# A two-layer graph kernel: projections as three float32r passes instead of seven-product float32 blocks

## The chip, the cores and the metric

The kernel runs on one core of one Trainium2 chip. The metric is the device time of one execution in microseconds (us): the median of three runs before the change is 3069.6 us. A core has five engines that work through queues of their own and wait for each other by semaphores. TensorE (PE in the profile, PEld for its weight loads) multiplies matrices into PSUM. VectorE (DVE), ScalarE (ACT) and GpSimd (POOL) work elementwise. SyncE (SP) issues most of the DMAs.

## The reference, cut to what matters

```python
# x: (64, 256, 512) float32; adj: (256, 256) of 0 and 1
# layer 0: a graph layer
mi = einsum('bkd,od->bko', x, Wi); mj = einsum('bkd,od->bko', x, Wj)
h  = layernorm(x + deg * (mi + b) + einsum('ij,bjo->bio', adj, mj))
# layer 1: attention of 8 heads of 64, masked by adj
q, k, v = h @ Wq.T + bq, h @ Wk.T + bk, h @ Wv.T + bv
attn = softmax(where(adj == 0, -inf, q @ k.T / 8))
out  = layernorm(h + (attn @ v) @ Wo.T + bo)
```

There are 64 elements in the batch. The two 512x512 weights of layer 0 and the four 512x512 projections of layer 1 are most of the arithmetic.

## The kernel before, in words

The kernel takes two elements at a time, so it has 32 groups (`NB` is 2, `NG` is 32), and `for g in range(NG - 1)` runs 31 times. The Python loop is unrolled: one iteration overlaps the attention of group g with layer 0 of group g + 1, and then with the output projection of g and the q, k and v projections of g + 1. Nothing is planned at run time. Matmuls, and whatever is wrapped in `in_order`, stay in the order in which the program emits them. The other instructions are emitted in the same place, and each engine takes its queue from the front.

**Layer 0** (`l0_steps`) makes the products of one element from seven block products (Strassen's scheme, in the form of Winograd). Each product is two float32 matmuls of 128x512. The blocks of x are turned on VectorE by `turn_x`, and their sums come from `sum_x`. The neighbour product (`neighbours`) multiplies the adjacency with `mj`, which was split into two float32r parts, `hi` by ScalarE and `lo` by GpSimd (`split`): eight float32r matmuls of 128x512. The layer norm is `norm_stats` on VectorE, a power on GpSimd (`rstd`) and `norm_apply` on ScalarE. `send_h` writes h to DRAM in columns and reads it back as `hB`, and `turn_h` turns it on VectorE.

**Projections.** `block_product` issues four float32 matmuls of 128x256. `pair_steps` uses it seven times for each of q, k, v and o, so that a projection of two elements takes 28 matmuls. VectorE makes the block sums that these products need (`hS`, `oS`), and it combines the products afterwards. The weight blocks stream in as 256 KB factors: `bring` issues the next one as soon as one has been used.

**Attention** goes over eight head pairs of a group. `scores` makes the scores of one pair: VectorE adds the mask, ScalarE takes exponentials, GpSimd adds the two halves into `pk`. `values` multiplies with v, `divide_two` makes denominators on PE (`den`), reciprocals on VectorE (`rden`), spreads them with eight small DMAs, and `multiply` applies them on GpSimd.

The end of an iteration sets the order of the work around the change:

```python
divide_two(g, w + 1)
run([o[0], neighbours, take1, take0, q[0], give1, send1, o[1], k[0], give0, send0, multiply,
     *left_steps(oS[g], in_order), q[1], k[1]])
run(o[2:6] + work[SLOTS + 2] + [v[0], o[6], v[1]])
```

Here `o[0]` is the first block product of the output projection, which stands ahead of the second element's neighbour product. In the last attention step before it, four layer 0 products of the second element (`q[3:7]`) stand between the scores and the values.

Of the kernel before, what the change touches and what calls it, by code (L numbers as in the profile page):

```python
# [16 lines left out]
P = 128  # L17
# [207 lines left out]
def unshifted_path(ctx, tc, flag, x, adj, wiT, wjT, b0, wqT, bq, wkT, bk, wvT, bv, woT, bo, out):  # L225
# [27 lines left out]
    AHEAD = 8  # L253
# [6 lines left out]
    p4 = ctx.enter_context(tc.tile_pool(name="p4", bufs=4))  # L260
    p6 = ctx.enter_context(tc.tile_pool(name="p6", bufs=6))
    stream = ctx.enter_context(tc.tile_pool(name="stream", bufs=AHEAD + 1))
# [35 lines left out]
    def load_x(b):  # L298
        if b < B:
            xh[b] = p6.tile([P, NT, D], F32, tag="xh", name="xh")  # L300
            nc.sync.dma_start(out=xh[b], in_=x[b].rearrange("(t p) d -> p t d", p=P))

    b_bc = p4.tile([P, D], F32, tag="u", name="b_bc")
# [20 lines left out]
    xT, xS, hT, hS, qT, kT, vv, aoT, oS = ({} for _ in range(9))  # L324


    ident = const.tile([P, P], F32, name="ident")
# [15 lines left out]
    aT = p3.tile([P, NT, N], F32, tag="pk", name="aT")  # L343
    deg = small.tile([P, NT], F32, tag="deg", name="deg")
# [16 lines left out]
    def check_graph():  # L361


        exact = p1.tile([P, NT, N], F32, tag="oS", name="exact")
        in_order(nc.vector.tensor_tensor(exact, aT, graph.bitcast(F32), ALU.not_equal))
        in_order(nc.vector.tensor_reduce(inexact, exact.rearrange("p t n -> p (t n)"), AX.X, ALU.max))
        in_order(nc.vector.tensor_scalar(maskT, aT, 0.0, MASK, ALU.is_equal, ALU.mult))
# [9 lines left out]
    def load_bias(b, name):  # L377
        t = const.tile([P, NC], F32, tag=name, name=name)
        nc.sync.dma_start(out=t, in_=b)
        d = const.tile([P, 2], F32, tag=name + "d", name=name + "d")  # L380
        return t, d

    bq_sb, bqd = load_bias(bq, "bq")
    bk_sb, bkd = load_bias(bk, "bk")

    def bias_steps():
        for t, d in ((bq_sb, bqd), (bk_sb, bkd)):
            in_order(nc.vector.tensor_sub(d, t[:, 2:4], t[:, 0:2]))

    bv_t = small.tile([P, NC], F32, tag="bvt", name="bv_t")  # L390
# [5 lines left out]
    def blocks_of(w):  # L396
        return (w.rearrange("(h c p) (j o) -> p h c j o", h=2, p=P, j=2) if w is woT else
                w.rearrange("(p h c) (j o) -> p h c j o", h=2, p=P, j=2))

    sources = {}  # L400
    for name, w in (("wq", wqT), ("wk", wkT), ("wv", wvT), ("wo", woT)):
        src = blocks_of(w)
        sources[name] = {B11: src[:, 0, :, 0], B21: src[:, 1, :, 0], B22: src[:, 1, :, 1]}


    def load_raw(w, tag):
        raw = p1.tile([P, 2, 2, 2, H], F32, tag=tag, name="raw")
        nc.sync.dma_start(out=raw.rearrange("p h c j o -> p (h c) (j o)"),
                          in_=w.rearrange("(c p) o -> p c o" if w is woT else "(p c) o -> p c o", p=P))
        return raw  # L410

    def make_factors(w, name, raw):
        kept = dram.tile([4, P, 2, H], F32, tag=name, name=name)
        t1, t2, t3, t4 = (p4.tile([P, 2, H], F32, tag="u", name="t") for _ in range(4))
        b11, b12, b21, b22 = (raw[:, h, :, j, :] for h in range(2) for j in range(2))
        for n, (t, p, m) in enumerate(((t1, b12, b11), (t2, b22, t1), (t3, b22, b12), (t4, b21, t2))):
            in_order(nc.vector.tensor_sub(t, p, m))
            nc.sync.dma_start(out=kept[n], in_=t)
        sources[name].update({T1: kept[0], T2: kept[1], T3: kept[2], T4: kept[3]})

    spread = p3.tile([P, NC, P], F32, tag="pk", name="spread")
# [3 lines left out]

    def fold_value_bias(raw):

        pb = score_bank("pb")
        for c in range(NC):
            h, kc = divmod(c, 2)  # L430
            matmul(pb, spread[:, c], raw[:, h, kc].rearrange("p j o -> p (j o)"),
                   start=(c == 0), stop=(c == NC - 1))
        nc.vector.tensor_add(bo_bc, pb, bo_bc)
# [4 lines left out]
    def bring():  # L438
        if queue:
            name, n = queue.pop(0)  # L440
            f = stream.tile([P, 2, H], F32, tag="factor", name="factor")
            nc.sync.dma_start(out=f, in_=sources[name][n])
            coming.append(f)

    def next_factor():
        f = coming.pop(0)
        bring()
        return f


    def norm_stats(t, order=anywhere):
# [3 lines left out]
        nc.vector.bn_aggr(mv, st)  # L455
        ve = small.tile([P, 1], F32, tag="ve", name="ve")
        nc.vector.tensor_scalar(ve, mv[:, 1:2], EPS, None, ALU.add)
# [3 lines left out]
        nc.gpsimd.tensor_tensor(rstd, ve, mhalf, ALU.pow)  # L461
# [40 lines left out]
    def l0_steps(b, late=False):  # L502
# [21 lines left out]
        def split(t):  # L524
            nc.scalar.copy(k["hi"][:, t, :], k["mj"][:, t, :])
            nc.gpsimd.tensor_tensor(k["lo"][:, t, :], k["mj"][:, t, :], k["hi"][:, t, :].bitcast(F32),
                                    ALU.subtract)

        def step1():
            product("x", raw(0, 0), B11, True)  # L530
            nc.scalar.copy(keeper("u1"), banks["x"])

        def step2():
            product("w", raw(1, 1), T4, True)
            add_scaled(1, banks["w"])

        def step3():
            product("x", raw(0, 1), B21, False)
            add_scaled(0, banks["x"])

        def step4():
            product("y", xS[b]["S2"], T2, True)
            nc.vector.tensor_add(keeper("u2"), banks["y"], k["u1"])

        def step5():
            product("z", xS[b]["S1"], T1, True)
            k["mj"] = p1.tile([P, NT, D], F32, tag="mj", name="mj")
            nc.vector.tensor_copy(k["mj"][:, 1, :], banks["z"])

        def step6():  # L550
            product("y", xS[b]["S3"], T3, False)
            nc.vector.tensor_add(keeper("u3"), banks["y"], k["u1"])
            nc.gpsimd.tensor_tensor(k["mj"][:, 1, :], k["mj"][:, 1, :], k["u3"], ALU.add)
# [21 lines left out]
        def take(t):  # L575
            r = xh[b][:, t, :]
            if late and t == 1:
                in_order(add_scaled(1, k["u3"]))
            in_order(nc.vector.tensor_add(r, k["pa"][:, t, :], r))
            stats[t] = norm_stats(r, in_order)  # L580

        def give(t):
            norm_apply(xh[b][:, t, :], *stats[t], in_order)


        return [step1, step2, step3, step4, step5, step6, step7, neighbours, lambda: take(1), lambda: take(0),
                lambda: give(1), lambda: send_h(b, 1), lambda: give(0), lambda: send_h(b, 0)]

    def new_h(g):
        hT[g] = p1.tile([P, NC, NB * N], F32, tag="hT", name="hT")  # L590
        hS[g] = pair_blocks(hT[g], "hS")

    def sum_h(g):
        for step in left_steps(hS[g], in_order):
            step()
# [3 lines left out]
    def send_h(b, t):  # L599
        i = b % NB  # L600
        if t == 1:
            h_cols[b] = dram.tile([D // P, N, P], F32, tag=f"h{i}", name="h_cols")
        nc.sync.dma_start(out=h_cols[b][:, t * P:(t + 1) * P, :].rearrange("q p n -> p q n"),
                          in_=xh[b][:, t, :].rearrange("p (q n) -> p q n", n=P))
        if t == 0:
            hB[b] = p1.tile([P, N // R, P], F32, tag="hB", name="hB")
            nc.sync.dma_start(out=hB[b].rearrange("p a n -> p (a n)"),
                              in_=h_cols[b].rearrange("q (r a) n -> (q r) (a n)", r=R))

    def turn_h(b):  # L610
        g, i = divmod(b, NB)
        if i == 0:
            new_h(g)
        transposed(hT[g][:, :, i * N:(i + 1) * N], hB.pop(b))
        if i == NB - 1:
            sum_h(g)

    def h_transpose(b, t, borrow=False):
# [499 lines left out]
```

## Time and profile before

| what | value |
|---|---|
| median of three runs | 3069.6 us (3069.17 to 3071.52) |
| the profiled execution: own time, span | 3068.79 us, 3066.9 us |
| granted TensorE clock | 0.999 |
| PE, PEld busy | 99%, 69% |
| DVE, ACT, POOL busy | 71%, 32%, 50% |
| DMA share, all 16 engines (queue q1) | 48.8%, 444.5 MB |
| one group, start to start | 94.39 us (1513.37 to 1607.76) |

The span runs from the first to the last instruction, and the execution's own time lies 1.9 us above it. An instruction group of the profile is given as line, engine, operation, output and inputs, count, busy time and mean duration. Ends of matmuls are modelled and overlap, so the time that a matmul really takes is read from the distance of two starts.

### The profile page before, as it was taken

Reading aid. Unit: us, or ns where it says so; the run is one execution under the profiler, and the core shown is the slowest. Engines: PE = TensorE matmul, PEld = TensorE weight load, DVE = VectorE, ACT = ScalarE, POOL = GpSimd, SP = SyncE. Lnnn points to the kernel's source line nnn. Section 1 sums busy time; section 2 is a strip of 40 time slices with the busy share of each in tenths; the row PEclk is TensorE's granted clock in tenths of the full one; section 3 lists DMA queues with packets and bytes.
Section 4 is the critical chain, followed back from the end, with each engine's and each line's share of the span. In section 5 each row is a group of like instructions: output and inputs, shape, how many; then the busy total and the mean of one; then the engine's idle time right before and its main releaser. Section 6 shows DMA issues by size and latency. Waiting matters only on the chain. (4 is left out here: it accounts for less than half of the span.)

```text
span 3066.9 us, 46810 instructions
## 1 busy us (share of the span) xinstructions
PE 3036.6 (99%) x16646; PEld 2124.6 (69%) x16646; DVE 2178.3 (71%) x3298; ACT 974.1 (32%) x1861; POOL 1519.5 (50%) x1255
## 2 busy tenths in 40 slices
PE   7999999999999999999999999999999999999998
PEld 4667766677766777666776667776677766677665
DVE  6776677766777667777677777677766777767775
ACT  2323333323333333332233332333333333323332
POOL 2544545544545445464454554454544546445453
PEclk9999999999999999999999999999999999999999
DMA  7455544455444555345553445544455444555333
GB/s 255 123 151 159 169 121 136 132 161 166 144 125 127 159 170 155 116 133 154 161 168 119 126 145 160 167 134 134 127 158 170 151 121 128 159 161 166 120 111 96
DMA packets 410411, 447.54 MB, mean 146 GB/s; under 512 B 40896, under 2 KB 300224, under 8 KB 409792
## 3 DMA queue, kind: packets, MB, share of 16 engines
q1 hardware_dynamic: 410176, 444.50, 48.8%
q8 instruction: 136, 2.23, 0.3%
q14 instruction: 99, 0.81, 0.1%
HBM read 340.79 MB, written 70.25 MB: 134 GB/s over the span
## 5 line engine op out<-in xcount | busy, mean ns | idle before, releaser
L461 POOL TENSOR_TENSOR rstd<-ve,mhalf 128x1 f32<-128x1 f32 x256 | 140.5, 552 | 707.3 <-DVE below L459 707.3
L816 POOL TENSOR_TENSOR pk<-pe 128x512 f32<-128x512 f32 x256 | 323.1, 1278 | 322.2 <-ACT pe L813 322.2
L290 PE MATMUL po<-w,xS 128*128 128x512 f32 x1024 | 462.2, 599 | 0.7 <-DVE xS L478 0.7
L290 PE MATMUL st<-hS,factor 128*128 128x256 f32 x2048 | 453.2, 379 | 1.5 <-DVE u L689 1.2
L290 PEld LDWEIGHTS st<-hS,factor 128*128 128x128 f32 x2048 | 388.4, 190 | 56.3 <-DVE xh L744 1.7
L813 ACT ACTIVATE pe<-pe 128x1024 f32<-128x1024 f32 x256 | 270.8, 1058 | 364.4 <-DVE pe L809 364.4
L290 PE MATMUL po<-w,xT 128*128 128x512 f32 x768 | 352.1, 601 | 14.8 <-DVE xS L477 9.3
L290 PE MATMUL st<-hT,factor 128*128 128x256 f32 x1536 | 352.5, 379 | 0.7 <-ACT hT L626 0.7
L290 PEld LDWEIGHTS po<-w,xS 128*128 128x128 f32 x1024 | 189.6, 190 | 235.6 <-issue 206.3
L809 DVE TENSOR_TENSOR pe<-ps,maskT 128x1024 f32<-128x1024 f32 x256 | 298.0, 1195 | 35.4 <-PE ps L290 35.4
L290 PEld LDWEIGHTS st<-hT,factor 128*128 128x128 f32 x1536 | 291.9, 190 | 41.8 <-ACT hT L626 0.9
L886 DVE RECIPROCAL rden<-den 128x256 f32<-128x256 f32 x127 | 222.5, 1752 | 76.6 <-PE den L290 73.6
L290 PEld LDWEIGHTS po<-w,xT 128*128 128x128 f32 x768 | 144.2, 191 | 181.9 <-issue 162.8
L887 POOL TENSOR_TENSOR rtot<-rtot,rden 128x256 f32<-128x256 f32 x127 | 106.8, 841 | 320.1 <-DVE rden L886 320.1
L290 PE MATMUL ps<-qT,kT 64*128 64x256 f32 x2048 | 265.0, 393 | 0.0
L290 PE MATMUL pav<-pe,v_sb 128*32 128x256 f32 x4096 | 248.4, 382 | 1.9 <-ACT pe L813 1.9
L290 PEld LDWEIGHTS ps<-qT,kT 64*128 64x128 f32 x2048 | 184.5, 186 | 78.1 <-issue 38.6
L744 DVE TENSOR_TENSOR xh<-st,xh 128x512 f32<-128x512 f32 x186 | 144.5, 777 | 132.2 <-PE st L290 132.2
L290 PE MATMUL st<-factor,hS 128*128 128x256 f32 x1024 | 234.8, 382 | 0.0
L290 PEld LDWEIGHTS pav<-pe,v_sb 128*32 128x32 f32 x4096 | 119.8, 110 | 164.3 <-issue 95.4
L290 PE MATMUL st<-factor,oS 128*128 128x256 f32 x992 | 224.2, 379 | 0.0
L290 PEld LDWEIGHTS st<-factor,hS 128*128 128x128 f32 x1024 | 192.1, 190 | 35.2 <-issue 10.6
(115 smaller groups left out, 4648.2 us busy)
## 6 DMA issues: line engine op xcount, KB each, us to landing
xB<-in_x_dram SPq DMA_DIRECT2D x256, 128.0 KB, 3.9
xh<-in_x_dram SPq DMA_DIRECT2D x64, 512.0 KB, 4.2
factor<-wq SPq DMA_DIRECT2D x128, 256.0 KB, 4.2
factor<-wk SPq DMA_DIRECT2D x128, 256.0 KB, 2.8
factor<-wv SPq DMA_DIRECT2D x128, 256.0 KB, 2.6
spread<-rden SPq DMA_DIRECT2D x1016, 32.0 KB, 1.9
factor<-wo SPq DMA_DIRECT2D x124, 256.0 KB, 3.2
h_cols<-xh SPq DMA_DIRECT2D x124, 256.0 KB, 3.0
```

Of the source, the lines that this page charges most:

```text
L290: in_order(nc.tensor.matmul(*args, **kw))
L461: nc.gpsimd.tensor_tensor(rstd, ve, mhalf, ALU.pow)
L744: nc.vector.tensor_add(dst, src, dst)
L809: nc.vector.tensor_add(pe.rearrange("p j t q -> p j (t q)"), ps.rearrange("p j t q -> p j (t q)"), maskT.rearrange("p t q -> p (t q)").uns ...
L813: in_order(nc.scalar.activation(flat, flat, AF.Exp, scale=QSCALE, accum_out=etot[:, NB * g + i, pr:pr + 1]))
L816: nc.gpsimd.tensor_tensor(pk, pe[:, :, 0, :], pe[:, :, 1, :], ALU.add)
L886: nc.vector.reciprocal(rden, den)
L887: nc.gpsimd.tensor_tensor(rtot, rtot, rden, ALU.add)
```

## The change

The four projections of layer 1 no longer use seven block products. Each operand is split into a head that float32r holds and a small low part. Three float32r matmuls replace one float32 matmul: head by head and low by low into a bank X, and a difference by a difference into a bank Y. The result is X times a constant plus Y. The activations are split on the chip: `split_head` on ScalarE, `split_diff` on VectorE, `split_low` on VectorE or GpSimd. The weights are split once, in `make`, and kept in DRAM. A factor is now 128 x 3 x 512 numbers (768 KB), and six of them are in flight instead of nine of 256 KB. The block sums of h and of the attention output are gone.

Around the products the order changes too. The last attention step keeps two layer 0 products (`q[5:7]`) where four stood. The neighbour product of the second element follows the denominators with nothing between. After it come three layer 0 products of the group two on (`p[0]`, `p[1]`, `p[2]`), and then the output projection, which needs the split attention output.

```diff
-    AHEAD = 8
+    RING = 6
+    UP, DOWN, LIFT = 1 + 2.0 ** -12, 1 - 2.0 ** -13, 2.0 ** 12
...
-            f = stream.tile([P, 2, H], F32, tag="factor", name="factor")
-            nc.sync.dma_start(out=f, in_=sources[name][n])
+            f = stream.tile([P, 3, D], F32R, tag="factor", name="factor")
+            if first:
+                make(f, name, j)
+            else:
+                nc.sync.dma_start(out=f.bitcast(F32), in_=kept[name][j])
...
+            low = nc.vector if late and t == 0 else nc.gpsimd
+            order(low.tensor_tensor(k["lo"][:, t, :], k["mj"][:, t, :], k["hi"][:, t, :].bitcast(F32),
+                                    ALU.subtract))
...
+    def split_head(parts, src):
+        in_order(nc.scalar.activation(parts[0], src, AF.Identity, scale=DOWN))
+
+    def split_diff(parts, src):
+        in_order(nc.vector.scalar_tensor_tensor(parts[2], parts[0].bitcast(F32), UP, src, ALU.mult, ALU.subtract))
+
+    def split_low(parts, src, engine):
+        in_order(engine.tensor_tensor(parts[1], src, parts[0].bitcast(F32), ALU.subtract))
...
+    def rows_of_product(banks, parts, t, f, c):
+        X, Y = banks
+        head, low, diff = (d[:, c, t * P:(t + 1) * P] for d in parts)
+        first, end = c == 0, c == NC - 1
+        matmul(X, head, f[:, 0, :], start=first, stop=False, skip_group_check=True)
+        matmul(Y, diff, f[:, 2, :], start=first, stop=end, skip_group_check=True)
+        matmul(X, low, f[:, 1, :], start=False, stop=end, skip_group_check=True)
...
+            dst = store[g][:, m, :]
+            in_order(nc.scalar.activation(dst, X, AF.Identity, bias=bias[:, m:m + 1], scale=UP))
+            in_order(nc.vector.tensor_add(dst, Y, dst))
...
+            now, later = scores(g, w + 2), scores(g, w + 3)
+            now()
+            if w == NB * NC - 4:
+                head, = three(("qT",))
+                split_head([head[:, :, :N]], aoT[g][:, :, :N])
+            later()
...
+            else:
+                run(q[5:7])
         w = NB * NC - 2
         values(g, w)
         values(g, w + 1)
+        diff, low = three(("kT", "v"))
+        aoP[g] = head, low, diff
+        split_low(*ao_parts(g, 0, every), nc.gpsimd)
         multiply()
...
+        rden = divide_two(g, w + 1)
+        nb2()
+        add2(1)
+        add2(0)
+        split_head(*ao_parts(g, 1, upper))
+        stat2(1)
+        split_diff(*ao_parts(g, 0, every))
+        split_low(*ao_parts(g, 1, upper), nc.gpsimd)
+        if g + 2 < NG:
+            p, q = layer0(g + 2)
+            p[0][0]()
+        give2(1)
+        send_h(b2, 1)
+        multiply()
+        stat2(0)
+        split_head(*ao_parts(g, 1, lower))
+        give2(0)
+        send_h(b2, 0)
+        split_diff(*ao_parts(g, 1, upper))
+        if g + 2 < NG:
+            run(p[0][1:3])
...
+        o = o_steps(g, "SMAS", [lambda: split_three(*turn_h(b2, 1), nc.vector),
+                                lambda: split_three(*turn_h(b2, 0), nc.vector)])
+        o[0]()
+        split_three(*turn_h(b1, 1), nc.gpsimd)
+        o[1]()
+        split_three(*turn_h(b1, 0), nc.gpsimd)
+        run([o[2], v[0], v[1], v[3], v[2], end[0], q_[0], end[1], k[0], end[2], q_[1], end[3], k[1], end[4]])
```

The letters in `o_steps` and `projection_steps` say which PSUM banks X and Y take: S both halves of one of the two score tiles, M two of the three common banks, A one common bank and the bank of the values.

## The prediction

> **What bounds the kernel now.** I read the page first: busy shares, slices, costliest groups. Then the timeline of one group from the middle, the windows over it, and the waits.
>
> ```profile
> PE 3036.6 (99%) x16646; PEld 2124.6 (69%) x16646; DVE 2178.3 (71%) x3298; ACT 974.1 (32%) x1861; POOL 1519.5 (50%) x1255
> ...
> PE   7999999999999999999999999999999999999998
> ```
>
> TensorE is busy from the second slice to the last. In the middle its order repeats every 94.39 us (start of the first layer 0 product at 1513.37, the same at 1607.76), and in that window PE is busy for all of it, DVE for 67.34, ACT for 30.33, POOL for 47.49. So the others cost nothing today, and every microsecond off PE's stream counts, if nobody else makes PE wait. PE's timeline at the end of the attention:
>
> ```profile
> 1553.02 1.93 PE L290 MATMUL pav<-pe,v_sb 128*32 128x256 f32 x32
> 1554.77 0.62 PE L290 MATMUL den<-pk,ones 128*32 128x256 f32 x8
> 1555.32 1.99 PE L290 MATMUL st<-factor,aoT 128*128 128x256 f32 x8
> 1556.96 0.58 PE L290 MATMUL pa<-hi,graph 128*128 128x512 f32 x1
> 1557.38 0.39 PE L290 MATMUL pa<-lo,graph 128*128 128x512 f32 x1
> 1557.61 0.40 PE L290 MATMUL pa<-hi,graph 128*128 128x512 f32 x1
> 1557.84 0.39 PE L290 MATMUL pa<-lo,graph 128*128 128x512 f32 x1
> ```
>
> Two prices are here. The float32r matmuls of the neighbour product start 0.2345 us apart. A float32 block product (eight records) takes 1.727 us, by the starts of 24 records in 5.18 us. And this neighbour product is just in time, as POOL's timeline shows:
>
> ```profile
> 1548.26 2.50 POOL L816 TENSOR_TENSOR pk<-pe 128x512 f32<-128x512 f32 x2 [1.47 <-ACT pe L813]
> 1552.18 1.27 POOL L553 TENSOR_TENSOR mj<-mj,u 128x512 f32<-128x512 f32 x1 [1.42 <-DVE u L552]
> 1554.18 2.53 POOL L526 TENSOR_TENSOR lo<-mj,hi 128x512 fp32r<-128x512 f32 x2 [0.73 <-ACT hi L525]
> ```
>
> The second low part ends at 1556.7, the product starts at 1556.96. POOL is half idle on average and has no slack here.
>
> **What the Trainium skill says.** "FP8 and Floating Point Precision" (TensorE Precision Notes): true float32 takes four passes[...]. "TensorE: Matmul & The Clock Gate" (Back-to-back issue gap) gives N/2.4 + 2.5 ns, 216 ns at 512 columns. The float32 records agree (two passes of 256 columns in 1.727/8 = 0.216); the float32r matmul does not: 0.2345, 9% more, and I use that. "VectorE: DVE Perf Modes" (The TRN2 errata) gives (N+151)/0.96 ns for a float32 tensor_tensor, 691 at 512; the trace has 686 to 692. "GPSIMD Engine Reference" (Specifications) says that GpSimd shares its SBUF interfaces with VectorE, which contends with instructions of two SBUF inputs. Sums of one shape (128x256) take 418 and 946 ns on different lines here, so I price VectorE's new work between these ends.
>
> **The change, part by part, for one group.**
>
> *Products.* 28 block products leave: 28 x 1.727 = 48.36 us. 4 projections x 48 float32r matmuls come: 192 x 0.2345 = 45.02. That is **-3.34**. Scores, values, layer 0 and neighbour products keep their number; three layer 0 products only move. Were each pass 0.216, the gain would be 6.9.
>
> *Sums and splits.* VectorE loses eight block sums (0.69 each), the combinations of q, k, v, and seven adds of o; it gains 12 bank adds of 0.69, eight adds for o (4 x 0.744 + 4 x 0.687), four half-size turns (2.16/2 each), and splits of 0.7 to 0.95. By counts times the rows it goes from 67 to about 74 us, ACT from 30 to 37, POOL stays at 48. No total is over the period; what counts is where they stand.
>
> *The neighbour product of the second element.* Clock: 0 when PE starts the last pair of scores. Unhindered, PE has the scores (1.93), the two layer 0 products (2 x 1.72), values (1.75), denominators (0.6), and reaches the neighbour product at 7.7. Its second matmul needs the low part. The chain behind that, in the order in which the compiled queues have it:
> - VectorE: the turn of x (2.12) now ends about 0.7 after 0, then the reciprocal (1.75) to 2.5, two mask adds (1.145 each) to 4.8.
> - ACT: first exponential with its accumulator (1.25) to 4.9; then the new `split_head` of the first element, 128x1024, 1.06 by the exponential of that shape, to 5.95; only then the second exponential, to 7.2.
> - POOL: its `pk` (1.28) to 8.5; behind that in its queue the `mj` add (1.3) to 9.8.
> - ACT `hi` (0.6) to 10.4; POOL `lo` (1.27) to 11.65.
>
> PE would have needed `lo` at 8.0. It is **+3.6** late, in small waits (values for the exponential, denominators for `pk`, then `hi`, then `lo`). Before, `u` was ready early enough, four products and `o[0]` stood in between, and POOL did `pk` before `mj` without loss. The bounds: if the turn of x is early, the chain is 0.6 shorter and the wait 3.0; if POOL takes 1.5 for `mj` and 1.45 for `lo`, as some do, 4.0. Queued behind this on VectorE: the other `lo` waits for ACT's second `hi`, and the last reciprocal waits behind that `lo`, until 11.9 instead of 7.8.
>
> *The first element's neighbour product.* Its last `lo` stands behind two `pk` on POOL: ready at 20.4 on a clock where PE needs it at 20.15: **+0.25** (0 to 0.5).
>
> *The output projection.* After the neighbour product (13.3) the three layer 0 products cover 5.16, to 18.45. VectorE: reciprocal to 13.65, two adds (1.37), scaled add (0.95), statistics (1.05), difference of the first element (1.22, or 1.9 with contention): 18.2 to 18.9. Needed at 18.7: 0 to 0.2. The eight spreading DMAs, now four each on SP and ACT's queue, and the multiply (POOL, to 20.1) are in time for the second element at 24.1. They cost nothing as long as o's first half covers them.
>
> *v.* VectorE goes on: statistics, split, two scaled adds, split to 22.6; adds of o[0] 24.0; then, twice, turn (1.06), wait for ACT's cast (0.65), difference (0.75) and o's adds (1.43), the second difference at 30.4; then twice turn, wait, difference, low (3.15) and adds, to 39.5. PE needs the first element's first half at 29.75 and gets difference and POOL's low part 0.75 late; v's last step waits for the score tile that the last adds free at 39.5, 0.6 after PE is there. The hB loads sit in SP's queue behind a factor load, which itself waits for PE to release a factor in the second half of o (25.8); they land at about 30 by 3.5 us from issue, as VectorE comes for them. Together +1.35 to +1.75, and I take **+2.2**, because VectorE overlaps POOL there; 1.0 without contention, 4 if the DMAs are late.
>
> *DMA.* Factors go from 28 x 256 KB = 7.3 MB to 16 x 768 KB = 12.6 MB per group. In the projection stage (1555.3 to 1602.3) 198 GB/s took a share of 0.64, so some 310 GB/s are to be had; there about 14.5 MB come in 47 us, 309. That is the edge, but six factors wait in their buffers at the start, and in q and k each is issued 6 us or more ahead of its use. I take 0 beyond the 2.2; the bound is +2.
>
> *Start.* PE waits for the first four v weights to be split (about 1.65 us of VectorE each, 6.6); the first group's three projections take 2.5 less; the rest is equal: **+5** (-5 to +15). The end keeps its float32 products.
>
> **Sum.** -3.34 + 3.6 + 0.25 + 2.2 = +2.7 per group; x 31 = +84; +5: 3068.8 + 89 = 3158 for the profiled execution. That execution is 0.8 below the median, so I say **3158** for the median too.
>
> **Rivals.**
> 1. *The neighbour product isn't late* (faster). Place: the chain exponential, `pk`, `mj`, `hi`, `lo`. If POOL's `mj` and ACT's `hi` got ahead of the second exponential's followers, the 3.6 would go, and with 1.35 in v the group gains 1.5: 3068.8 - 46 + 5 = 3028; with no wait left, 3068.8 - 104 + 5 = 2970. The point where it decides: all waits of a group under 3.3 us. For it: PE is the only full engine. Against it: the compiled queues put `mj` behind both `pk`, and all durations are from this trace.
> 2. *Passes at 0.216* (faster or equal). 6.9 gained against 6.05 lost: -0.85 x 31 + 5, 3047. Against it: all float32r bursts of the trace run at 0.2345.
> 3. *DMA or contention holds PE* (slower still). v and o wait another 2: 3158 + 62 = 3220. For it: 309 against 310 GB/s. Against it: the ring.
>
> **Chances.** My forecast (3090 to 3190) 0.52; rival 3, above 3190, 0.20; rivals 1 and 2 together 0.23; between them 0.05. Within 0.2% (6 us, about what a measurement of this kernel can tell from no change) is a narrow band: 0.05. Slower 0.72, faster 0.23. The range reaches to 3240 (neighbour 4.0, tail 4, start +15 give 3068.8 + 31 x 5.1 + 15 = 3242) and down to 3010, half of the faster cases; the forecast's own range is 3090 to 3190.
>
> **What would show it.** Right: the period is about 97 us; `pa` waits 3 to 4 us per group for `hi` and `lo` (line of the split); PE is busy for 93 to 95%; new products 0.2345 apart; v's last step waits for VectorE's adds of o. Wrong: PE at 98 to 99% and a period of 91 to 92 (rival 1); passes at 0.216 (rival 2); factor DMAs as releasers of PE (rival 3).

## The result, and the profile after

The changed kernel takes **3306.36 us** (median of four runs, 3301.79 to 3315.72), the kernel before 3069.39 beside it: ratio 1.0775, interval 1.0751 to 1.08. It is slower by 237 us, where the forecast said 88 and its range ended at 3240. The sign was right, the size was not.

The page after, its part 1 and a row of part 2:

```profile
PE 3032.3 (92%) x15630; PEld 1958.5 (59%) x15630; DVE 2488.4 (75%) x3411; ACT 1150.3 (35%) x2022; POOL 1581.7 (48%) x1221
...
PE   7899989999989999999999999899999899999988
```

PE is busy for 92%, not 99%, and yet as many microseconds as before (3032 against 3037) with 1016 matmuls fewer. Part of its busy time is spent at a lower clock: the mean granted clock is 0.972, before it was 0.999. The waits of PE's weight loads (line, releaser: us in total, times, longest) say where the idle time is; before, no row but "issue" had over 21 us in all:

```profile
PEld pxy L290 <- DMA factor<-wv: 109.7, 31, 4.3
PEld pa L290 <- POOL lo L525: 67.7, 62, 1.2
...
PEld pa L290 <- ACT hi L523: 53.5, 31, 1.7
PEld po L290 <- ACT u L530: 47.5, 31, 3.5
```

`pxy`, `px` and `py` are the banks X and Y; `hA`, `hL` and `hD` are head, low part and difference of h, and for the attention output these three lie in the tiles `qT`, `v` and `kT`. The `u` of line 530 is the copy that frees the bank of a layer 0 product.

**The neighbour product of the second element**, PE's timeline, in the place of the one shown of before:

```profile
1573.90 2.04 PE L290 MATMUL pav<-pe,v_sb 128*32 128x256 f32 x32
1575.76 1.09 PE L290 MATMUL den<-pk,ones 128*32 128x256 f32 x8
1578.10 0.50 PE L290 MATMUL pa<-hi,graph 128*128 128x512 f32 x1 [1.24 <-ACT hi L523]
1579.44 0.80 PE L290 MATMUL pa<-lo,graph 128*128 128x512 f32 x1 [0.85 <-POOL lo L525]
1580.04 0.63 PE L290 MATMUL pa<-hi,graph 128*128 128x512 f32 x1
1580.46 0.63 PE L290 MATMUL pa<-lo,graph 128*128 128x512 f32 x1
```

POOL's timeline for the same stretch:

```profile
1572.91 1.28 POOL L779 TENSOR_TENSOR pk<-pe 128x512 f32<-128x512 f32 x1 [1.53 <-ACT pe L776]
1574.89 1.28 POOL L779 TENSOR_TENSOR pk<-pe 128x512 f32<-128x512 f32 x1 [0.71 <-ACT pe L776]
1576.13 1.26 POOL L555 TENSOR_TENSOR mj<-mj,u 128x512 f32<-128x512 f32 x1
1578.12 1.27 POOL L525 TENSOR_TENSOR lo<-mj,hi 128x512 fp32r<-128x512 f32 x1 [0.73 <-ACT hi L523]
```

This is the predicted chain: `pk`, `mj` behind it, `hi`, `lo`. The last scores start at 1568.35, so the clock of the prediction has `lo` ready at 11.04, where it said 11.65. PE's second matmul starts at 11.09; the prediction had 8.0 for an unhindered PE, so this one is 3.1 us late, where it said 3.6. What it did not say stands in the last two rows of PE: after the waits the matmuls follow 0.42 us apart, where the same ones before the change were 0.2345 apart.

**The projection of v.** PE's timeline around the longest wait of a group:

```profile
1499.49 0.40 PE L290 MATMUL pxy<-factor,hL 128*128 128x512 f32 x1
1503.55 0.51 PE L290 MATMUL pxy<-factor,hA 128*128 128x512 f32 x1 [3.66 <-DMA factor<-wv]
...
1504.54 0.63 PE L290 MATMUL px<-factor,hA 128*128 128x512 f32 x1
1504.97 0.63 PE L290 MATMUL py<-factor,hD 128*128 128x512 f32 x1
1505.39 0.63 PE L290 MATMUL px<-factor,hL 128*128 128x512 f32 x1
...
1507.53 0.40 PE L290 MATMUL py<-factor,hD 128*128 128x512 f32 x1
1507.76 0.40 PE L290 MATMUL px<-factor,hL 128*128 128x512 f32 x1
```

The windows view over these places (window, its length, busy time and instructions of PE, PEld, DVE, ACT, POOL, granted clock, DMA share, GB/s):

```profile
1499.50:1503.30 3.80, 0.39 (x2) 0.00 (x0) 3.17 (x5) 0.56 (x1) 0.00 (x0) 1.00 0.99 383
1504.50:1507.50 3.00, 3.00 (x8) 2.31 (x7) 2.97 (x5) 0.60 (x1) 0.00 (x0) 0.50 0.09 39
1507.50:1510.50 3.00, 3.00 (x15) 2.45 (x14) 0.86 (x2) 0.60 (x1) 0.00 (x0) 1.00 0.00 0
...
1580.00:1582.60 2.60, 2.60 (x8) 1.99 (x6) 1.76 (x1) 0.00 (x0) 2.60 (x2) 0.50 0.01 3
```

While PE waits, the DMA engines are full (share 0.99, 383 GB/s). After the wait the clock is 0.50 in a window of 3 us, and PE does 8 matmuls where it then does 15. In this profile such half clock follows 24 of the 31 factor waits and 19 of the 31 waits at the neighbour product. The Trainium skill, "TensorE: Matmul & The Clock Gate" (What's actually happening), has the array at half rate after an idle window of some 3.4 us and at full rate after a busy one. The wait of 3.66 us would fit this. But 10 of the 24 factor waits with half clock behind them are shorter than 3.41 us (the shortest 1.95), and at the neighbour product PE had been idle for only 1.24 and 0.85 us with a matmul between them, so an idle stretch of the window's length is not needed.

What decides can be worked out from this trace. In its record of the clock, 45 of the 50 stretches at half clock last 3.41 us, four more two or three times that, and all of them start on one grid of this step. Divide the profile along this grid, without its first 130 us and its last 120: PE is idle for more than 1.86 us in 35 of the 897 windows, and half clock follows each of them. It follows none of the 850 windows with less than 1.69 us, and 7 of the 12 between. So some half a window of idle time is enough, in one piece or in several, if it falls into one window. The two waits of the neighbour product are the same in every group, 2.09 us together; half clock follows where at least 1.69 us of them fall into one window (19 groups), and not where an edge cuts them so that no window has more than 1.59 (12 groups). The factor waits divide in the same way: with half clock behind them one window has 1.87 us or more, without it none has over 1.86. Two windows around the wait of 3.66 us, and two around a factor wait of 2.29 us that an edge cuts:

```profile
1500.70:1504.11 3.41, 0.56 (x2) 0.48 (x3) 3.02 (x5) 0.32 (x1) 0.00 (x0) 1.00 0.95 389
1504.11:1507.52 3.41, 3.41 (x9) 2.63 (x8) 3.03 (x5) 0.91 (x2) 0.00 (x0) 0.50 0.14 58
...
1599.68:1603.10 3.42, 2.09 (x8) 1.24 (x7) 1.82 (x3) 0.63 (x1) 0.79 (x1) 1.00 0.95 347
1603.10:1606.51 3.41, 1.82 (x8) 1.52 (x9) 2.93 (x5) 0.41 (x1) 0.00 (x0) 1.00 0.99 411
```

The first window has 2.85 us without PE, and the next one half clock; the last two have 1.33 and 1.59, and PE keeps its clock behind them.

Why the factor is late is seen in SP's queue (its timeline, the issues of DMAs), one group on:

```profile
1595.00 0.33 SPq L428 DMA_DIRECT2D factor<-wv  x1
1597.98 0.81 SPq L626 DMA_DIRECT2D hB<-h_cols  x2
1598.88 0.38 SPq L428 DMA_DIRECT2D factor<-wv  x1
1599.35 0.38 SPq L428 DMA_DIRECT2D factor<-wq  x1
1599.83 0.38 SPq L428 DMA_DIRECT2D factor<-wk  x1
```

There is one `hB` buffer. The `hB` loads of the second element wait until VectorE has turned the first element's second half (that turn ends at 1597.94), and all factors behind them in the queue wait too. The waits of SP have this as a row, 31 times 2 us:

```profile
SPq L626 <- DVE hF L483: 62.7, 31, 2.7
```

Two halves of h and three factors then go out within 2 us of each other and share the engines; the page gives a wv factor a median of 7.3 us from issue to landing (2.6 before, at 256 KB).

**The balance.** The span grows by 246.9 us. The first product with v (`pav`) starts at 125.37, before at 103.63: 21.7 for the start. From there to the last `pav` it is 3167.1 instead of 2943.8: 223.3, or **+7.2 in each of 31 groups**, where the prediction had +2.7.

| per group, us | predicted | measured |
|---|---|---|
| products: 192 passes for 28 block products | -3.34 | -4.8 (passes 0.2267 apart) |
| second neighbour product | +3.6 | +2.1 idle (`hi` 1.25, second `lo` 0.85) |
| first neighbour product | +0.25 | +0.6 idle |
| layer 0 products and output projection | 0 to 0.2 | +0.8 idle (`u`) |
| v, with the DMA's 0 | +2.2 | +3.1 (factor) and 0.4 (`hL`) |
| half clock | none | +2.6 |
| the rest of the waits of over 0.1 us | none | +0.6 |

The idle column counts from modelled ends of matmuls. By starts each wait costs 0.2 to 0.3 more (in the last run below, 1.14 us from one start to the next, where 0.23 is the step, show as 0.64 of idle): some 1.3 for six waits. Half clock is put at 0.028 of 3314 us, 93 in all, as if PE had had work in all of it; 12 of it lie in the start. The column adds up to 6.7 with this 1.3; the last 0.5 I have not followed.

### The profile page after: what moved, and what is told of

It is laid out like the page before. It is cut to its first block, busy times and chain, and to the rows that moved or that the text cites. A ratio compares the mean times of both kernels' runs of the same rounds, so it can differ in the third digit from the quotient of the medians.

```text
span 3313.8 us, 43898 instructions
## 1 busy us (share of the span) xinstructions
PE 3032.3 (92%) x15630; PEld 1958.5 (59%) x15630; DVE 2488.4 (75%) x3411; ACT 1150.3 (35%) x2022; POOL 1581.7 (48%) x1221
## 5 line engine op out<-in xcount | busy, mean ns | idle before, releaser
L459 POOL TENSOR_TENSOR rstd<-ve,mhalf 128x1 f32<-128x1 f32 x256 | 169.8, 667 | 816.1 <-DVE below L457 816.1
L690 DVE TENSOR_TENSOR kT<-py,kT 128x512 f32<-128x512 f32 x128 | 88.0, 688 | 186.3 <-ACT kT L689 186.3
L599 ACT ACTIVATE hA<-hF 128x512 fp32r<-128x512 f32 x124 | 78.3, 631 | 388.9 <-DVE hF L483 388.9
L465 ACT ACTIVATE xh<-xh,shift,rstd 128x512 f32<-128x512 f32 x256 | 208.8, 816 | 8.6
L290 PE MATMUL pxy<-factor,hA 128*128 128x512 f32 x256 | 106.0, 414 | 100.2 <-DMA factor<-wv 96.4
L810 POOL TENSOR_TENSOR aoT<-aoT,spread 128x512 f32<-128x512 f32 x127 | 182.9, 1440 | 24.5 <-DMA spread<-rden 15.8
L605 POOL TENSOR_TENSOR v<-aoT,qT 128x512 fp32r<-128x512 f32 (+1 forms) x93 | 182.9, 1966 | 7.3 <-ACT qT L599 7.3
L483 DVE STREAM_TRANSPOSE hF<-hB 128x512 f32<-128x512 f32 x124 | 138.5, 1117 | 53.6 <-DMA hB<-h_cols 53.6
L451 DVE BATCH_NORM_STATS2 st<-xh 128x6 f32<-128x512 f32 x256 | 175.4, 685 | 1.2
L290 PE MATMUL px<-hA,factor 128*128 128x512 f32 x640 | 175.1, 395 | 0.0
```

The costliest lines, as they stand in the source:

```text
L290: in_order(nc.tensor.matmul(*args, **kw))
L451: order(nc.vector.bn_stats(st, t))
L459: order(nc.gpsimd.tensor_tensor(rstd, ve, mhalf, ALU.pow))
L465: order(nc.scalar.activation(t, t, AF.Identity, bias=shift, scale=rstd))
L483: in_order(nc.vector.transpose(dst.rearrange("p c (n a) -> p a c n", n=R), blocks.rearrange("p a (r c) -> p a c r", c=NC)))
L605: in_order(engine.tensor_tensor(parts[1], src, parts[0].bitcast(F32), ALU.subtract))
```

## The experiments

All times are medians beside runs of the kernel before on the same chip (medians of 3067.87 to 3070.05). In the expectations, theory V says that from the last `pk` to the end of v the chain over VectorE, ScalarE and GpSimd sets the time; its rivals put it on the factors' DMAs or on PE's own waits.

**1. Is it the factor wait?** Three kernels: the `hB` half that blocks the queue is loaded later, behind the factors; a factor brings only its first third (the low parts of the weights are left out, all passes use the head); dummy matmuls stand in front of v.

```diff
-            for u in (1, 0):
+            for u in (1, 0) if i == 0 else (1,):
...
-        o = o_steps(g, "SMAS", [lambda: split_three(*turn_h(b2, 1), nc.vector),
+        o = o_steps(g, "SMAS", [lambda: (load_hB(b2, 0), split_three(*turn_h(b2, 1), nc.vector)),
```

> The changed kernel, with each half of hB as a tile of its own (two buffers, the same bytes) and the load of the second element's second half moved behind the factor loads that the output projection releases. Theory A (SP's queue is blocked: the second v factor stands behind an hB load that waits for VectorE to free the only hB buffer): the factor is issued some 2.8 us earlier, PE's wait for it (3.1 us per group) falls under 0.5, and the half-clock stretch behind it (about 1.4 us lost) goes with it: 31 x 4 = 125 us less, about 3180. Theory B (bandwidth: 768 KB factors cannot land in time whatever the order): the wait stays over 2 us, within 25 us of 3306.

```diff
-                nc.sync.dma_start(out=f.bitcast(F32), in_=kept[name][j])
+                nc.sync.dma_start(out=f[:, 0, :].bitcast(F32), in_=kept[name][j][:, 0, :])
```

> The changed kernel, with factors of a third of the bytes: only the head of each weight is loaded, and all three passes use it (so the low parts of the weights are left out of the result); matmuls, DMA count and queue order are the same. Theory A: the late issue stays, but 256 KB land in about 3 us instead of 5, so PE's wait for the v factor falls from 3.1 to about 1 and the half clock partly stays: 60 to 120 us less, 3190 to 3250. Theory B: all waits for factors go and 125 us or more are gained, 3180 or below, clearly better than the reordering alone.

```diff
             X, Y = banks = pair(kind)
+            for _ in range(2 if g and (i, t) == (0, 0) else 0):
+                for c in range(2):
+                    rows_of_product(banks, hP[g], 0, coming[c], c)
```

> The changed kernel, with twelve extra float32r matmuls (2.75 us) ahead of the first v product of each group, into its own banks, overwritten by its start. They move the wait for the late v factor from 3.1 us of idle to some 0.5. Theory A (idle time throttles the clock, and behind this wait PE is the bound): the half-clock stretch behind it (seven matmuls at 0.427 for 0.227, 1.4 us) goes, 31 x 1.4 = 43 us less, about 3260. Rival C (the clock costs nothing, since VectorE's chain sets the end of v anyway): within 10 us of 3306.

Measured: 3359.2 (1.0922 to 1.0958), 3227.3 (1.0493 to 1.0528) and 3274.6 (1.0657 to 1.0693). The later `hB` load made the kernel 53 us slower, not faster: the factor wait fell from 3.1 to 1.3 us per group, but PE then waited 2.7 for VectorE's adds of o, which free the score bank (`xh`), as the prediction's step for v had said. With a third of the bytes the factor wait is gone, 79 us come back (of the 87 between the two profiles 39 are half clock, by the same reckoning as in the balance), and the same bank costs 1.4. The twelve dummies add work for PE and make the kernel 32 us *faster*, with the clock at 0.986: PE works in what was the factor wait (0.5 left) and keeps its clock. So the half clock behind a wait is a cost of its own.

**2. Is it the neighbour product's wait?** The head cast behind both exponentials; ten dummy matmuls ahead of the product; one of the three layer 0 products moved ahead of it.

```diff
             now()
+            later()
             if w == NB * NC - 4:
                 head, = three(("qT",))
                 split_head([head[:, :, :N]], aoT[g][:, :, :N])
-            later()
```

> The changed kernel, with the head cast of the attention output's first element moved on ScalarE from between the last two exponentials to behind them. Theory A (the chain exponential, pk, mj, hi, lo sets the neighbour product): the chain is 1.05 us shorter, PE's waits before and in the neighbour product fall from 2.1 (hi, lo) by 1.05 per group: 33 us less, up to 75 if the half clock behind it goes too; 3230 to 3275. Rival: the reciprocal and VectorE's splits set the output projection, the wait moves there and nothing is gained, 3300 to 3310.

```diff
         def neighbours(fill=0):
             k["pa"] = score_banks("pa")
+            for _ in range(fill):
+                matmul(k["pa"][:, 1, :], graph[:, 1, P:2 * P], coming[0][:, 0, :], start=True, stop=True)
```

> The changed kernel, with ten extra float32r matmuls of 128x512 ahead of the second element's neighbour product, into the same bank, overwritten by its start (2.3 us of PE time inside the wait for hi and lo). Theory A (the idle time throttles PE's clock to half, which costs about 1.4 us behind it): PE gets 2.3 us more work per group and the group is 1.5 us shorter, 46 us less, about 3260. Rival C (the slow matmuls behind the wait are held by something else than the clock): no change, or up to 30 us more.

```diff
         rden = divide_two(g, w + 1)
+        if g + 2 < NG:
+            p, q = layer0(g + 2)
+            p[0][0]()
         nb2()
```

> The changed kernel, with one of the three layer 0 products moved from behind the second neighbour product to ahead of it. If PE is the bound there (the prediction's reckoning), its wait for hi and lo falls from 2.1 to 0.4 per group, 31 x 1.7 = 53 us less, about 3255. Theory V (from the last pk to the end of v the chain over POOL, ScalarE and VectorE sets the time, and PE's waits are only where its slack shows): the wait comes back at the layer 0 products or at the output projection, within 12 us of 3306.

Measured: 3294.7 (1.0719 to 1.0754), 3295.8 (1.0716 to 1.0752) and 3350.6 (1.0904 to 1.094). The later head cast took 0.15 us off the wait for `hi`, not 1.05. The dummies took the second neighbour product's waits away and raised the clock to 0.984, and only 11 us came of it (the intervals just touch): the wait for `u` rose from 0.8 to 1.65 us. With real work in the gap it rose to 2.8, and the kernel was slower by 44. All of PE's idle time grew by only 0.2 us per group there, but more of it comes in one piece, and the clock fell to 0.963: of the 32 us between the two profiles, half clock makes up 31. So work put into this gap made the next wait longer: PE alone did not set the time of this stretch.

**3. Both ends of v.** VectorE adds o's bank before it turns h; first with a third of the bytes (low parts left out), then with whole factors and the first two v steps interleaved, so that each factor serves two tiles and is needed later.

```diff
-                between[t]()
                 add(1, t, banks[t])
+                between[t]()
...
-        run([o[2], v[0], v[1], v[3], v[2], end[0], q_[0], end[1], k[0], end[2], q_[1], end[3], k[1], end[4]])
+        run([o[2], v_two(g + 1, "SM"), v[3], v[2], end[0], q_[0], end[1], k[0], end[2], q_[1], end[3], k[1], end[4]])
```

> As the run with a third of the factor bytes (low parts of the weights left out), and VectorE adds each bank of the second half of o before it turns h, not after. Theory V: VectorE, idle for the hB load there, frees the score tile some 2 us earlier, the wait of v's last step for that tile (1.44 us per group in the run with a third of the bytes) falls under 0.4, 35 us less than that run: about 3190. Rival (the hB load sets VectorE's end, and the adds fit only behind it): within 10 us of 3227.

> The changed kernel with full factors, the first two v products of each group interleaved chunk by chunk (so that the late v factors are needed 1.4 us later), and VectorE's adds of o before its turns of h. If both the late factor and VectorE's adds hold v: the wait for the factor falls from 3.1 to about 1.7, the half clock behind it mostly goes, and v's last step doesn't wait instead: 2.4 us per group, 75 us less, about 3230. If only the factor's landing counts and VectorE is next: 20 to 30 us less. If neither: 3306.

Measured: 3175.4 (1.0335 to 1.0369) and **3217.0** (1.0457 to 1.0492). Interleaving and the adds in front give 89 us with every byte loaded: the factor wait is 1.2, the bank's wait gone.

**4. The chain: `mj` ahead of the last `pk`, `hi` and the head cast after the last exponential; the last spreads all on SP; both; both with a third of the bytes** (low parts left out). The three kernels with `mj` early also issue one step of the start twice: for the second element of the first group half of `mj` is split again, and `u3` (times deg) is added to its x once more, so that this element comes out wrong. The last of the four has v interleaved, other than the kernel of 3175 us that is its base.

```diff
             now()
             if w == NB * NC - 4:
+                q[5]()
+            later(in_order if w == NB * NC - 4 else anywhere)
+            if w == NB * NC - 4:
                 head, = three(("qT",))
-                split_head([head[:, :, :N]], aoT[g][:, :, :N])
-            later()
...
-                run(q[5:7])
+                run([q[7], q[6]])
+                split_head([head[:, :, :N]], aoT[g][:, :, :N])
```

> On top of the interleaved v products and the earlier adds (3217 us): the second element's mj add stands ahead of the last pk on GpSimd, its hi cast follows the last exponential, and the head cast of the attention output stands behind both. Theory V: the chain pk, mj, hi, lo, reciprocal is some 2.3 us shorter per group, PE's waits for hi and lo fall from 2.1 to about 0.5, and the reciprocal behind lo comes earlier, so that o and v follow: 50 to 70 us less, 3145 to 3165. If the late v factor takes over (it is released by PE, so it moves along), still 40 us or more. If the neighbour product's waits are slack: within 10 us of 3217.

> On top of the interleaved v products and the earlier adds (3217 us): all eight spreading DMAs of the last head pairs are issued by SP again, none by ScalarE. ScalarE's queue is then free 2.7 us earlier (four issues of 0.68), so the copy u that the third layer 0 product waits for (0.8 us per group) is no longer late: 25 us less, 3192. Rival: SP needs as long for the four, the last multiply comes later and o's second half waits instead: within 10 us of 3217, or more.

> The two last edits together, on top of the interleaved v products and the earlier adds. Theory V: the gains add up, 3120 to 3150, with PE idle for some 3 us per group (the late factor, hL, the first neighbour product, qT). If one wait takes the other's place: no better than the better of the two alone.

> The same, with factors of a third of the bytes (low parts of the weights left out). What the float32r passes give once neither the factors nor the vector chain hold PE: the group comes to 93 to 95 us against 94.4 before, total 3060 to 3110. If it stays over 3140, waits that no run has touched hold the change back.

Measured: 3240.5 (1.0545 to 1.058), 3234.2 (1.0524 to 1.0559), 3226.3 (1.0491 to 1.0526) and 3202.0 us (1.0412 to 1.0447): none gains on its base (3217, and 3175 for the last), all four expectations of a gain missed. PE's weight loads and VectorE in the first of them show why:

```profile
PEld po L290 <- ACT u L530: 115.6, 32, 5.0
PEld pa L290 <- POOL lo L525: 47.0, 62, 1.0
```

```profile
DVE rden L871 <- DMA spread<-rden: 31.5, 15, 4.4
```

The `hi` wait is gone and `lo` is down from 67.7. But the last reciprocal waits for the spreading DMAs of the pair before it (in its base such waits come to 18.7 us in all, the longest 1.6), since the change had cut `rden` to a single buffer. In the last of the four kernels SP issues the sixteen spreads one after the other in 13.32 us, and VectorE's timeline has

```profile
1530.18 1.76 DVE L871 RECIPROCAL rden<-den 128x256 f32<-128x256 f32 x1 [2.06 <-DMA spread<-rden]
```

In the first kernel ScalarE has four of the last pair's spreads behind that reciprocal (0.68 us each in its queue), and behind them the copy of `u`, which frees the bank that PE's next layer 0 product needs: 2.8 us of waiting per group, 0.8 in its base. With the spreads on SP that wait is gone, but PE waits elsewhere instead: for parts of h in v, and with both edits also for the difference of the attention output in o (35.6 us in all).

**5. Is the single `rden` buffer the link?** Two buffers for `rden` and `spread` need 3 KB that only a smaller ring gives; so first the ring alone, from the version of 3217 us; then two buffers; then `mj` early; then two buffers with a third of the bytes (low parts left out) and `mj` late.

```diff
-    RING = 6
+    RING = 5
...
-        rden = p1.tile([P, N], F32, tag="rden", name="rden")
+        rden = p2.tile([P, N], F32, tag="rden", name="rden")
...
-        pool, tag = (p3, "lu") if last else (p1, "spread")
+        pool, tag = (p3, "lu") if last else (p2, "spread")
```

> The version with the first two v steps interleaved and o's adds ahead of the turns (3217 us), with five factor buffers instead of six. That frees 6 KB per partition, which the next two runs need. It is their base. Theory V (the chain over VectorE, ScalarE and GpSimd from the last pk to the end of v sets the time): the sixth buffer is worth little, 3210 to 3235. Theory D (the factor stream sets the time): a factor comes one use later, 3250 to 3300.

> The same, with two buffers each for the reciprocals (rden) and for what they are spread into, as before the change; the change had left one of each. Theory V, with the single buffer as a link of the chain: the last reciprocal no longer waits until the spreading DMAs of the pair before it have read its buffer (0.5 to 2 us in over half of the groups), so 15 to 40 us below the run with five factor buffers. Theory D, or V with other links that bind: within 5 us of it.

> The same with the two buffers and, as in the run before that was slower for it, the mj add ahead of the last pk on GpSimd and the head cast behind the high part. Then it cost 23 us. If the single rden buffer ate the gain, it is now no slower than the run with two buffers, and up to 60 us faster. If the late pk is the cause (it releases the denominators and so the reciprocal and the output projection), it is again 15 to 30 us slower.

> Only the head's third of each factor is loaded and used in all passes (the low parts of the weights are left out), o's adds stand ahead of the turns, five factor buffers, two buffers for the reciprocals and their spread. With one buffer and six factors it took 3175 us. Theory V with the single buffer as a link: 3120 to 3160. Other links bind: 3170 to 3180.

Measured: 3300.7 (1.0738 to 1.0767), 3290.4 (1.0709 to 1.0743), **3240.9** (1.054 to 1.0569) and 3174.3 (1.0328 to 1.0356). The sixth factor buffer is worth 84 us: with five, two v factors instead of one stand behind the `hB` loads, and the factor wait is back at 2.85. The second `rden` buffer alone is worth about 10 (the intervals just touch), and nothing with a third of the bytes. But with it `mj` early gains 50, where it had lost 23 without (with six factor buffers; with five and one `rden` buffer it was not run). The two edits are one: the first late link hid the second.

**6. With six factors.** The last reciprocal of a group gets a slot of `lu`; `mj` early, the adds of o in front; whole factors and interleaved v, then a third of the bytes (low parts left out) with v as in the changed kernel.

```diff
-        rden = p1.tile([P, N], F32, tag="rden", name="rden")
+        rden = (p3 if last else p1).tile([P, N], F32, tag="lu" if last else "rden", name="rden")
```

> Six factor buffers again, the first two v steps interleaved, o's adds ahead of the turns, mj ahead of the last pk, the head cast behind the high part; and the last reciprocal of a group has a buffer of its own (a slot of lu). Without that buffer this took 3240 us, and 23 us less with mj behind the last pk. With five factor buffers, and two for the reciprocals, mj early was worth 50 us. So if the single rden buffer was what turned the gain round, now 3150 to 3185, and the wait of the layer 0 product for u falls from 2.8 to about 0.7 us per group. If it was not: 3220 to 3245.

> The same three edits of the order (o's adds ahead, mj early, own buffer for the last reciprocal), the v steps one after the other, and only the head's third of each factor loaded and used in all passes (the low parts of the weights are left out). It takes the factor wait, the long wait of the second neighbour product and the rden buffer away together. Without mj early and the own buffer 3175 us. If these three and the half clock behind them are the loss, 3100 to 3140, still above the kernel before; if half clock remains behind what waits are left, 3150 to 3175.

Measured: **3162.7** (1.0299 to 1.0327) and **3105.3** (1.0108 to 1.0139), both as expected of the buffer as the link; the wait for `u` is 0.7 us per group in the first, as expected too. Of the 63 us between the profiles of the kernel of 3217 us and of this first one, half clock makes up some 36. POOL in the first of them has `mj` ahead of the second `pk`:

```profile
1501.91 1.27 POOL L796 TENSOR_TENSOR pk<-pe 128x512 f32<-128x512 f32 x1 [1.53 <-ACT pe L793]
1503.14 1.28 POOL L555 TENSOR_TENSOR mj<-mj,u 128x512 f32<-128x512 f32 x1
1504.38 1.27 POOL L796 TENSOR_TENSOR pk<-pe 128x512 f32<-128x512 f32 x1
1505.61 1.29 POOL L525 TENSOR_TENSOR lo<-mj,hi 128x512 fp32r<-128x512 f32 x1
```

and PE passes from the denominators to the neighbour product with 0.20 of idle time, at full clock:

```profile
1506.26 0.49 PE L290 MATMUL pa<-hi,graph 128*128 128x512 f32 x1
1506.96 0.50 PE L290 MATMUL pa<-lo,graph 128*128 128x512 f32 x1 [0.20 <-POOL lo L525]
1507.29 0.40 PE L290 MATMUL pa<-hi,graph 128*128 128x512 f32 x1
```

The mean granted clock is 0.994 in both profiles. In the one with whole factors, half clock follows 1 of the 23 factor waits of over 1 us. The two differ in the factors' bytes and in the order of v, so the 57 us between them are only about what the bytes still cost (1.25 us of wait per group and what hangs on it). In the second a group takes 94.7 us against 94.39 before: the passes' gain of 4.8 just pays for 3.3 of small waits, their 1.2 by starts, and the rest. Its other excess is the start, 19.7 us to the first `pav` (123.36 against 103.63). No version beat the kernel before.

## Why the prediction was right or wrong

- **Right: the sign and its mechanism.** The gain of the passes is smaller than the waits that the new order and the new operands bring. The neighbour product's chain held: every link came, in the order given, 0.4 to 0.8 us earlier than said. `pa` waits as forecast, 3.1 us of the 3.6 by the starts of its matmuls (2.1 as idle time). What came on top is the half clock behind it.
- **Wrong: the DMA step.** "I take 0 beyond the 2.2; the bound is +2" failed: PE waits 3.1 us for a factor, and 3.5 in all of v. The prediction had the `hB` loads behind a factor and asked whether they come in time for VectorE. It did not ask what stands behind *them*: they wait for VectorE to free their buffer and hold SP's queue for 2 us. "Six factors wait in their buffers" failed with it, for a new factor is issued only as one is used, and those of v's end are issued in o. The rate was underrated too: 310 GB/s was taken from a share of 0.64 in proportion, 383 at 0.99 was measured. Rival 3 had the sign to look for (factor DMAs as releasers of PE) and a price of 62 us; the later runs give the factors' part as more than that: two thirds of the bytes left out gave 79.
- **Wrong: no term for the clock.** The sum priced a wait at its length. Half clock after waits cost some 93 us in this execution, as much as the whole forecast loss. The kernel before hardly ever waited once it had started, at 0.999, so its profile showed no price. The Trainium skill, "TensorE: Matmul & The Clock Gate" (HAM oscillation), describes a kernel that loses its clock at every DMA wait of some 3 to 5 us. The forecast had 3.6 and 2.2 us of waits in every group; half clock behind both belonged into its bounds. Without the 2.6 of half clock the 7.2 per group would be some 4.6, and the range reached to 5.1.
- **Wrong: "they cost nothing"** of the spreads. Four of them in ScalarE's queue take 2.7 us ahead of a copy that frees a bank for PE, and they start only after a reciprocal that has lost its second buffer. The prediction followed the operands and missed the buffer counts in the diff. The `u` wait of 0.8 is the small visible part; the runs of parts 4 to 6 show that this link hid the gain of `mj` early. The repairs of part 2 were not run again without it.
- **v's VectorE steps: right, but covered.** The wait of v's last step for the adds of o was not there in the changed kernel. It was behind the factor wait, and came out at 1.4 to 2.7 as soon as that went.
- **The passes: better than predicted.** 0.2345 held for the first ten or so of a burst, then 0.2267. All bursts before were of eight. (The trace before has VectorE's adds of 128x512 from 666 to 692 ns, not from 686; no sum of the prediction hangs on it.)
- **The start: +5 predicted (-5 to 15), 21.7 measured.** Some 10 are idle time (PE waits 3.1 and 1.6 us for the first split factors, 2.5 for a layer norm, 2.6 for a sum of v), some 10 half clock after it.

## What to carry to other kernels

When a change adds waits to an engine that never waited, price each at its length and, for TensorE, add the half clock that can follow. In these profiles it comes where the idle time in one window of 3.41 us passes some 1.7 to 1.9 us, and then costs up to 1.7 more (half of 3.41). A wait brought under that is worth more than its length. Follow each queue in order past every instruction that waits for a buffer, a DMA issue too: what stands behind it waits as well, whatever its own operands. And read in the diff how many buffers each tile had and has: a single buffer can hide what another repair would gain, so a repair that gains nothing may still be half of the answer.

## What the runs showed of the hardware

- Half clock came not only after one wait of 3.66 us but in 19 of 31 cases after two of about 1.24 and 0.85 us. It came in windows of 3.41 us on one grid: behind all 35 windows of the changed kernel with more than 1.86 us of idle PE, behind none of the 850 with less than 1.69. The changed kernel and the 18 of the experiments together have 333 windows with 2 us or more, and half clock follows all of them; of 15,880 with less than 1.3 us it follows 19 (start and end of each profile left out as above). Idle time is taken here from modelled ends of matmuls, so the edge is not sharper than that.
- Matmuls with no use could keep half clock away: 12 of them in front of v made the kernel 32 us faster.
- float32r matmuls of 128x512, each with a weight load of its own, run 0.2345 us apart at the start of a burst and 0.2267 after some ten. At half clock they are 0.427 apart.
- A spread of 32 x 256 numbers takes 0.6 to 0.68 us of the issuing queue (four in 2.41 us on SP in the changed kernel, in 2.72 on ScalarE in the first kernel of part 4), a factor of 768 KB only 0.32 to 0.38.
